# Two graph layers on one core: contraction rows in another order, one row per step, and the second half of the gather ahead of the sums

## The chip, the cores and the metric

The program runs on one core of a Trainium2 chip. The metric is device time in microseconds (us) of one execution; lower is better. All operands are fp32.

## What is computed

```python
# N = 3327 nodes, D = 512; adj is dense in memory, [N, N]
h = relu(layernorm(x))                              # layer 0
q, k, v = h @ Wq.T + bq, h @ Wk.T + bk, h @ Wv.T + bv
x = x + softmax(q @ k.T / sqrt(D) + 2 * adj) @ v
h = relu(layernorm(x))                              # layer 1
A2 = adj + I
s = diagonal(A2) ** -0.5
x = x + relu((s[:, None] * A2 * s[None, :]) @ (A2 @ h @ W.T))
```

## The kernel before, in words

**Tiles.** The 3327 rows are padded to 26 tiles of 128. Large products are done by a Strassen scheme of seven products ("p1" to "p7", in the order p5, p1, p6, p7, p2, p3, p4, line 30), so both the contraction rows and the output columns are cut into halves. Columns stand in two strips (line 38): strip 0 has tiles 0 to 13, strip 1 tiles 14 to 25, and each strip has an upper half y=0 (7 or 6 tiles, 896 or 768 columns) and a lower half y=1. Contraction rows are tiles 0 to 12 in the first half and 13 to 25 in the second.

**Start (lines 266 to 374).** Each tile of x is normalised and transposed in four packs, its rows are stored to `rowd[0]`, and queries are projected and stored to `qd`.

**Scores (lines 379 to 568).** Four groups of 13 steps make exp(scores). Each step loads a tile row of adj (`adjacency`), and `sum_of_adjacency` also stores two sums of adj's quarters, with ones added on the diagonal (line 439), for the second layer. The order on DVE, PE, POOL and SP is the program's own there (`in_order`); what is issued outside it, such as the first loads of the layers, is placed by a planner that goes by estimated times.

**The three passes (lines 923 to 1039).** Pass g=0 is exp(scores) @ h, pass 1 is A2 @ h1, pass 2 is A2 @ temp. A pass is 7 products x 2 strips x 7 steps. The text writes a step as (g, product, strip, t), t = 0 to 5 or None; a product's strip is 896 or 768 columns wide and each matmul takes half of that, 448 or 384. Steps t = 0 to 5 multiply two contraction tiles at once by seven matmuls of one more Strassen level (`Step.multiply`, line 772); the odd thirteenth tile is step None, with four plain matmuls (line 764). PSUM has 8 banks: seven accumulate p1 to p7 of the inner level. Bank 3 serves the rows described below. In step None the fourth matmul, "p8", goes into p1's bank.

What step k of `run` (line 1006) issues, in order: the loads of step k+3 (SP queue); the matmuls of step k; on DVE the sums for step k+2 (`four_sums`, lines 170 to 172, three instructions); after t=5 `Gather.first` (lines 800 to 804), which copies p1 on ACT and empties p6, p7, p5 on DVE; in step None `Gather.rest` (lines 817 to 820), which empties p2, p3, p4 and p8 on DVE, and `settle` (lines 822 to 833), two DVE instructions for products p6, p2, p3, p4 and six for p7; then what `between` holds for the step. All five engines run in the order in which this is written. Step (…, 0) of the next product and strip starts each bank anew and so waits until `first` and `rest` have read it; its order is p6, p7, p5, p2, p3, p4, p1, and in other steps p1 comes first. The second matmul of those steps reads the third of the sums, written at line 171.

`between` holds: loads of the right operands five steps ahead (SP) and their differences three steps ahead (DVE, lines 176 to 179 and 734 to 740), for the first product p5 of passes 1 and 2 three and two steps ahead; `Job`s, 52 sums for later S2 and S4 (line 855); and the **rows**. A row of pass 0 is one finished output tile: four matmuls with Wv into bank 3 (line 864), on DVE x + product / total (876), + bias (877), statistics (190 to 194); a store of the new x by POOL (878); one step later the relu on ACT into an `h1` tile (883) and its store by POOL to `rowd[1]` (884). Its x tile is loaded one step ahead on ACT's queue (871) into one of three places; `h1` has two. A row of pass 1 is four matmuls with W (864), a scaling on ACT (892) and a store. Rows of pass 2 (`finish`) are transposed, scaled, added to x and stored out (917 to 920).

**When rows come before.** Outputs of the upper half y=0 are final after product p3, those of y=1 after p4. Rows 0 to 3 stand in steps (g, p3, 1, 2 to 5), rows 4, 5, 6, 14, 15, 16 in (g, p4, 0, 0 to 5), rows 7; 8, 9; 10; 11, 12; 13 in (g, p4, 1, 1 to 5), two in one step twice, and rows 20 to 25 and 17 to 19 in every second step from (g+1, p5, 0, 0). Product p5 of the next pass needs contraction tiles 0 to 12 alone.

**Diagonal.** `left` (line 679) loads the left operand. For A11, A12 and A22 of passes 1 and 2 it comes from adj, and ones are added on its diagonal by DVE right behind the load's issue (line 696), three steps before use.

Of the kernel before, what the change touches and what calls it, by code (L numbers as in the profile page):

```python
# [15 lines left out]
P = 128  # L16
# [19 lines left out]
HALF = 13  # L36
PAIRS = 6
STRIPS = (0, 14)
HT = (7, 6)
H = tuple(n * P for n in HT)  # L40
Q = tuple(n * P // 2 for n in HT)


@with_exitstack
def graph_layers_kernel(
# [28 lines left out]
    nc = tc.nc  # L74
# [193 lines left out]

    def load_x(i, queue=nc.sync):
        xt = x_ring([P, D], "xt")  # L270
        queue.dma_start(xt, x[i * P : (i + 1) * P])
        return xt

    order = [(k, t + y * HALF) for k in TURN for t in range(PACKS[k][0], sum(PACKS[k])) for y in range(2)]
# [36 lines left out]
    def h_transposed(k):  # L311

        a, n = PACKS[k]
        for _, i in (o for o in order if o[0] == k):
            xt = first.pop(i) if i in first else load_x(i)
            rstd, bias = norm(xt)
            ht = n_ring([P, D], "ht")
            nc.scalar.activation(ht, xt, AF.Relu, bias=bias(), scale=rstd)
            nc.gpsimd.dma_start(rowd[0][i], ht)
            pt = tp_bank("tp").rearrange("p (c e) -> p c e", c=DC)  # L320
            for c in range(DC):
                nc.tensor.transpose(pt[:, c], ht[:, c * P : (c + 1) * P], ident)
            w = slice((i % HALF - a) * P, (i % HALF - a + 1) * P)
            if i < HALF:
                nc.scalar.copy(hp[k][:, 0:2, :, w], pt.rearrange("p (a c) e -> p a c e", a=2))
            else:
                nc.scalar.copy(hp[k][:, 2, :, w], pt[:, 2:4])
                nc.vector.tensor_add(hp[k][:, 3, :, w], hp[k][:, 2, :, w], pt[:, 0:2])
                nc.vector.tensor_add(hp[k][:, 5, :, w], hp[k][:, 0, :, w], pt[:, 0:2])
        nc.vector.tensor_add(hp[k][:, 4], hp[k][:, 3], hp[k][:, 0])  # L330
        nc.vector.tensor_add(hp[k][:, 6], hp[k][:, 1], hp[k][:, 4])

    def project_q(k):
        a, n = PACKS[k]
        w = n * P

        qs = [half(8 + j, [P, 2, BW], "qs") for j in range(4)]

        def chain(o):
            def product(ps, name, start):  # L340
                for c in range(2):
                    nc.tensor.matmul(ps[:, :w], M[B[name]][:, c, o * P : (o + 1) * P], hp[k][:, A[name], c],
                                     start=start and c == 0, stop=c == 1, skip_group_check=True)

            def first(j, ps, sign):
                d = 2 * (j % 2) + o
                nc.scalar.activation(qs[j][:, o, :w], ps[:, :w], AF.Identity, bias=u[:, d : d + 1], scale=float(sign))

            def more(j, ps):
                nc.vector.tensor_add(qs[j][:, o, :w], qs[j][:, o, :w], ps[:, :w])  # L350

            def last():
                if o == 1:
                    for j in range(4):
                        y, z = divmod(j, 2)
                        i = (y * HALF + a) * P
                        nc.gpsimd.dma_start(qd[:, 2 * z : 2 * z + 2, i : i + w], qs[j][:, :, :w])

            Chain(product, first, more, last)

        for o in range(2):
            chain(o)
# [43 lines left out]
    def adjacency(s, q, t):  # L406

        wd, c = Q[s], q * Q[s]
        g = [take([P, 2, Q[0]], f"g{k}")[:, :, :wd] for k, take in enumerate(g_rings)]
        for k in range(2):  # L410
            r0, c0 = (k * HALF + t) * P, STRIPS[s] * P
            src = adjT[r0 : r0 + P, c0 : c0 + 2 * H[s]].rearrange("p (y w) -> p y w", y=2)
            nc.sync.dma_start(g[k], src[:, :, c : c + wd])
        return g

    class Pair:
# [11 lines left out]
        def sum_of_adjacency(self, m):  # L428

            g, t, s = self.g, self.t, self.s  # L430
            if m == 0:
                self.o = o_ring([P, 2, Q[0]], "o")[:, :, : self.wd]
            o = self.o[:, m]
            parts = ((0, 0), (0, 1)) if m == 0 else ((1, 1), (0, 1))
            nc.vector.tensor_add(o, *(g[k][:, y] for k, y in parts))  # L435
            for k, y in parts:
                d = diagonal(o, (k * HALF + t) * P, STRIPS[s] * P + y * H[s] + self.c)
                if d:
                    nc.vector.tensor_add(o[:, d[0]], o[:, d[0]], d[1])
            if m == 1:  # L440
                nc.gpsimd.dma_start(self.to(sumd)[:, 0:2], self.o)  # L441
# [227 lines left out]

    spare = [(mid, k) for k in range(10, 15)]  # L670
    job_ring = ring(*spare[2:], (half, 14))
    h_ring = ring(*spare[:2])
    ts_ring = ring(*spare[:3])
    xr_ring = ring(*spare[:3], (half, 14))
    out_ring = ring((half, 12), (half, 13), *spare[3:])
# [3 lines left out]
    def left(g, s, what, t):  # L679


        js = [HALF - 1] if t is None else [t, t + PAIRS]
        a = a_ring().rearrange("p a w -> p (a w)")[:, : len(js) * H[s]].rearrange("p (k w) -> p k w", k=len(js))
        for k, j in enumerate(js):
            if g == 0:
                nc.sync.dma_start(a[:, k], pd[s][j][:, E_AT[what], :])
                continue
            if what in SUMS:
                nc.sync.dma_start(a[:, k], sumd[s][j][:, SUMS.index(what), :])
                continue  # L690
            y, z = int(what[1]) - 1, int(what[2]) - 1
            r0, c0 = (z * HALF + j) * P, STRIPS[s] * P + y * H[s]
            nc.sync.dma_start(a[:, k], adjT[r0 : r0 + P, c0 : c0 + H[s]])
            d = diagonal(a[:, k], r0, c0)
            if d:
                nc.vector.tensor_add(a[:, k, d[0]], a[:, k, d[0]], d[1])
        return a.rearrange("p k (y w) -> p k y w", y=2)

    class Right:

# [8 lines left out]
        def rows(self, dst, h, z):  # L709

            for k, i in enumerate(self.its):
                src = rowd[self.g][h * HALF + i]
                nc.sync.dma_start(dst[:, k], src if z is None else src[:, z * E : (z + 1) * E])

        def load(self):
# [29 lines left out]
    class Step:  # L745
# [3 lines left out]
            self.g, self.r, self.s, self.t, self.right = g, r, s, t, right  # L749

        def load(self):
            self.a = left(self.g, self.s, A_OF[self.r], self.t)

        def sums(self):
            if self.t is None:
                return
            self.o = o_ring3()[:, :, : Q[self.s]]
            four_sums(self.o, self.a.rearrange("p k y w -> p (k y) w"))
# [81 lines left out]
    class Job:  # L840
# [5 lines left out]
        def load(self):  # L846
            s, j, w = self.s, self.j, H[self.s]
            self.a, self.b = (job_ring([P, H[0]], "job")[:, :w] for _ in range(2))
            r0, c0 = (self.k * HALF + j) * P, STRIPS[s] * P
            nc.sync.dma_start(self.a, sumd[s][j][:, 1 + self.k])  # L850
            nc.sync.dma_start(self.b, adjT[r0 : r0 + P, c0 : c0 + w])
            self.d = diagonal(self.b, r0, c0)
# [14 lines left out]
    xts = {}  # L867

    def attend_load(i):
        xts[i] = view(2, 1).rearrange("p a w -> p (a w)")[:, len(xts) % 3 * D :][:, :D]  # L870
        nc.scalar.dma_start(xts[i], x[i * P : (i + 1) * P])

    def attend(i):
# [58 lines left out]
    def at(k, what, *args):  # L932
        between.setdefault(k, []).append((what, args))

    early = []
    for g in range(3):
        for n, r in enumerate(ORDER):
            for t, e in enumerate(every):
                k = number_of(g, n, 0, t)
                rh = rights[g, r, e]  # L940

                lead, make = (3, 2) if g and n == 0 else (5, 3)
                for what, when in ((rh.load, k - lead), (rh.make, k - make)):
                    if when < 0:
                        early.append(what)
                    else:
                        at(when, what)
# [8 lines left out]
    def rows(g, k, i, *z):  # L956

        if g == 0:
            at(k - 1, attend_load, i)
            at(k, attend, i)  # L960
            at(k + 1, attended, i)
        elif g == 1:
# [3 lines left out]
            at(k, finish, i, *z)  # L966


    for g in range(2):
        for t, i in {2: 0, 3: 1, 4: 2, 5: 3}.items():  # L970
            rows(g, number_of(g, 5, 1, t), i)
        for t, i in enumerate((4, 5, 6, 14, 15, 16)):
            rows(g, number_of(g, 6, 0, t), i)
        for t, its in {1: (7,), 2: (8, 9), 3: (10,), 4: (11, 12), 5: (13,)}.items():
            for i in its:
                rows(g, number_of(g, 6, 1, t), i)
        for k, i in enumerate((*range(20, 26), *range(17, 20))):
            rows(g, number_of(g + 1, 0, 0, 0) + 2 * k, i)
    within = {}
    for (n, s, t), its in {  # L980
# [25 lines left out]
    def run(k):  # L1006
# [13 lines left out]
        for j, _ in enumerate(step.multiply(banks_of)):  # L1020
            if j == 3 and t == PAIRS - 1 and gatherer.last:
                gatherer.first(banks_of)
            for what, args in within.get(k, ()) if j == 3 else ():
                what(*args)
        sums()
        if t == PAIRS - 1 and not gatherer.last:
            gatherer.first(banks_of)
        if t is None:
            gatherer.rest(banks_of)
            gatherer.settle()  # L1030
        for what, args in between.get(k, ()):
            what(*args)
# [382 lines left out]
```

## Time and profile before

| what | value |
|---|---|
| four runs | 2218.8, 2221.76, 2222.26, 2222.41 us; median 2222.01 |
| the profiled execution | 2222.17 us; span of its instructions 2220.3 us |
| granted TensorE clock, mean | 0.994 |
| DVE busy | 1618.5 us (73%) |
| ACT busy, POOL busy | 231.7 us (10%), 357.6 us (16%) |
| HBM traffic | 262 GB/s over the span |
| start and projections | 0 to about 120 us |
| scores | about 121 to 655 us |
| pass 0, 1, 2 | from about 642, 1158 and 1705 us |

In the profile, PE is the matmul engine and PEld its weight loads; an fp32 matmul leaves two records, so 14 records are one step of seven matmuls. A line of the timeline or of the groups gives start, duration, engine, source line, output<-inputs and count, and in brackets the idle time of that engine just before it and who ended it. DVE instructions overlap a little, so distances between starts are used below where a sum of work is meant.

### The profile page before, as it was taken

The page shows a single profiled execution, that of the slowest core. Times are in us where ns is not written, and L with a number is a line of the kernel's source. Part 1 is how long each engine was busy: PE and PEld are TensorE (multiplying, and loading weights), DVE is VectorE, ACT ScalarE, POOL GpSimd, SP SyncE. Part 2 cuts the span into 40 slices and gives each one's busy share as a digit, 9 for nine tenths or more (in the row PEclk, how much of TensorE's full clock was granted, in tenths as well). Part 3 has the DMA queues.
Part 4 walks back from the last instruction along what each step waited for, and adds up shares of the span by engine and source line. Part 5 has one row for each costly group of instructions (what it writes and reads, how often), then busy time and mean ns, then how long its engine had stood idle before and what let it go on. Part 6 is the DMA issues. An engine that isn't in the chain of part 4 may idle for free.

```text
span 2220.3 us, 20949 instructions
## 1 busy us (share of the span) xinstructions
PE 2179.7 (98%) x6268; PEld 1167.5 (53%) x6268; DVE 1618.5 (73%) x3092; ACT 231.7 (10%) x336; POOL 357.6 (16%) x551
## 2 busy tenths in 40 slices
PE   9999999999999999999999999999999999999997
PEld 5555555455555555555445555555554555555554
DVE  6369888788877789867767778986634457777675
ACT  5321111112110000000000000000000000000011
POOL 4223333333331000001222110000000000000011
PEclk9999999999999999999999999999999999999998
DMA  7568888888969898888787899886636458766684
GB/s 249 206 212 303 294 299 284 303 285 309 349 221 318 312 371 299 287 298 285 253 285 266 306 333 362 281 285 199 221 119 204 144 175 292 245 203 195 206 297 161
DMA packets 246682, 583.68 MB, mean 263 GB/s; under 512 B 34768, under 2 KB 106270, under 8 KB 246558
## 3 DMA queue, kind: packets, MB, share of 16 engines
q1 hardware_dynamic: 192270, 399.28, 54.2%
q0 software_dynamic: 44928, 167.49, 19.9%
q10 hardware_dynamic: 9360, 15.47, 2.1%
q8 instruction: 52, 0.85, 0.2%
q14 instruction: 72, 0.59, 0.1%
HBM read 414.28 MB, written 167.85 MB: 262 GB/s over the span
## 4 chain that ended last, share of the span: by engine, by line
PE 64%; DVE 3%; DMA 1%; issue 1%; ACT 0%; POOL 0%; ACTq 0%; SPq 0%; DVEq 0%; POOLq 0%
PE p L772 52%; PE p L864 8%; PE p L764 4%; DVE part L170 0%; PE pt L917 0%; DMA part<-in_x_dram 0%; DMA xr<-x1d 0%; DVE part L171 0%; DVE part L876 0%; DMA b<-row 0%; DVE part L172 0%; DMA rows<-row 0%; DMA part<-sum 0%; DVE st L190 0%; DVE part L877 0%
## 5 line engine op out<-in xcount | busy, mean ns | idle before, releaser
L772 PE MATMUL p<-part,b 128*128 128x448 f32 (+1 forms) x3528 | 1255.0, 514 | 7.9 <-DVE part L817 7.6
L772 PEld LDWEIGHTS p<-part,b 128*128 128x128 f32 x3528 | 668.8, 190 | 573.4 <-issue 307.1
L170 DVE TENSOR_TENSOR part<-part 128x896 f32<-128x896 f32 (+1 forms) x252 | 256.7, 1019 | 124.3 <-PE p L772 83.0
L449 PE MATMUL Y<-qt,hp 128*128 128x448 f32 (+1 forms) x832 | 309.0, 514 | 3.6 <-DVE g L453 2.6
L449 PEld LDWEIGHTS Y<-qt,hp 128*128 128x128 f32 x832 | 157.4, 190 | 139.1 <-issue 72.3
L449 PE MATMUL Z<-qt,hp 128*128 128x384 f32 (+1 forms) x416 | 162.6, 513 | 0.0
L172 DVE TENSOR_TENSOR part<-part,part 128x448 f32<-128x448 f32 (+1 forms) x219 | 129.5, 591 | 17.0 <-PE p L772 0.9
L171 DVE TENSOR_TENSOR part<-part,part 128x448 f32<-128x448 f32 (+1 forms) x219 | 129.4, 591 | 7.4
L864 PE MATMUL p<-w,ct 128*128 128x512 f32 x272 | 123.8, 594 | 3.9 <-DVE part L876 2.2
L764 PE MATMUL p<-part,b 128*128 128x448 f32 (+1 forms) x336 | 124.2, 513 | 0.0
L449 PEld LDWEIGHTS Z<-qt,hp 128*128 128x128 f32 x416 | 78.8, 190 | 67.4 <-issue 36.2
L453 DVE SCALAR_TENSOR_TENSOR g<-g,Y 128x384 f32<-128x384 f32 (+1 forms) x156 | 91.3, 585 | 27.3 <-PE Y L449 26.2
L858 POOL DMA_DIRECT2D sum<-job x52 | 28.4, 547 | 472.9 <-DVE job L855 260.7
L801 DVE TENSOR_TENSOR part<-p,part 128x384 f32<-128x384 f32 (+1 forms) x33 | 19.3, 586 | 103.9 <-PE p L772 103.3
L764 PEld LDWEIGHTS p<-part,b 128*128 128x128 f32 x336 | 63.6, 190 | 54.0 <-issue 33.0
L800 ACT COPY part<-p 128x384 f32<-128x384 f32 (+1 forms) x33 | 16.6, 503 | 682.3 <-PE p L772 681.5
L864 PEld LDWEIGHTS p<-w,ct 128*128 128x128 f32 x272 | 51.3, 190 | 64.7 <-issue 50.5
L449 PE MATMUL X<-qt,hp 128*128 128x384 f32 (+1 forms) x208 | 81.1, 512 | 0.0
L456 ACT ACTIVATE g<-g 128x768 f32<-128x768 f32 (+1 forms) x48 | 43.0, 896 | 352.0 <-DVE g L453 300.4
L441 POOL DMA_DIRECT2D sum<-o x52 | 36.9, 709 | 219.9 <-DVE o L435 153.9
L864 PE MATMUL p<-w,part 128*128 128x512 f32 x144 | 65.7, 592 | 0.0
L876 DVE SCALAR_TENSOR_TENSOR part<-p,rs,part 128x512 f32<-128x512 f32 x26 | 19.5, 750 | 62.9 <-PE p L864 47.3
(162 smaller groups left out, 1872.7 us busy)
## 6 DMA issues: line engine op xcount, KB each, us to landing
part<-sum SPq DMA_DIRECT2D x104, 448.0 KB, 4.9
part<-p SPq DMA_DIRECT2D x91, 448.0 KB, 6.2
part<-sum SPq DMA_DIRECT2D x104, 384.0 KB, 3.5
part<-p SPq DMA_DIRECT2D x91, 384.0 KB, 4.1
part<-in_adjT_dram SPq DMA_DIRECT2D x78, 448.0 KB, 4.7
b<-row SPq DMA_DIRECT2D x234, 128.0 KB, 4.8
part<-in_adjT_dram SPq DMA_DIRECT2D x78, 384.0 KB, 3.7
g<-in_adjT_dram SPq DMA_DIRECT2D x52, 448.0 KB, 4.6
```

What stands on the lines that cost most here:

```text
L170: nc.vector.tensor_add(o[:, 0:2], g[:, 0:4:3], g[:, 1:2].to_broadcast([P, 2, g.shape[-1]]))
L171: nc.vector.tensor_add(o[:, 2], o[:, 1], g[:, 0])
L172: nc.vector.tensor_add(o[:, 3], o[:, 2], g[:, 2])
L441: nc.gpsimd.dma_start(self.to(sumd)[:, 0:2], self.o)
L449: nc.tensor.matmul(ps[:, :wd], h_of(self.t, name, k), qt[B[name]][:, k], start=start and k == 0, stop=k == 1, skip_group_check=True)
L453: nc.vector.scalar_tensor_tensor(a[n], a[n], 2.0, ps[:, :wd], op0=ALU.mult, op1=ALU.add if sign > 0 else ALU.subtract)
L456: nc.scalar.activation(g[1], g[1], AF.Exp, **({"bias": pad} if self.t == HALF - 1 else {}))
L764: yield nc.tensor.matmul(ps[("p2", "p3", "p4", "p8")[k]][:, :w], b[:, z], a[:, 0, y], start=k == 3, stop=True)
L772: yield nc.tensor.matmul(ps[r][:, :w], b[:, i], m, start=self.t == 0, stop=self.t == PAIRS - 1 and r in ("p1", "p5", "p6", "p7"))
L858: nc.gpsimd.dma_start(sumd[self.s][self.j][:, 2 + self.k], self.a)
L864: nc.tensor.matmul(ps, cts[s][y][d][:, k * P : (k + 1) * P], w[d], start=d == 0, stop=d == DC - 1)
L876: nc.vector.scalar_tensor_tensor(xt, ps, rs[:, i : i + 1], xt, op0=ALU.mult, op1=ALU.add)
```

## The change

Five edits, all of them in the order of things; no matmul is added or removed.

```diff
+ROW = tuple(STRIPS[s] + y * HT[s] + k for y in range(2) for s in range(2) for k in range(HT[s]))
...
-        queue.dma_start(xt, x[i * P : (i + 1) * P])
+        queue.dma_start(xt, x[ROW[i] * P : (ROW[i] + 1) * P])
```

Contraction place i now stands for row tile `ROW[i]`: 0 to 6, 14 to 19 (all of y=0) in the first half, 7 to 13, 20 to 25 (all of y=1) in the second. Every address that names a contraction row (`rowd`, `qd`, adj's rows, the diagonal's place) goes through `ROW`.

```diff
-    h_ring = ring(*spare[:2])
+    x_slots = [lambda k=k: view(2, 1).rearrange("p a w -> p (a w)")[:, k * D : (k + 1) * D] for k in range(3)]
+    x_slots = itertools.cycle([*x_slots, lambda: mid(10, [P, D], "xt")])
+    h_ring = ring((mid, 11))
...
+        diagonals = []
...
             if d:
-                nc.vector.tensor_add(a[:, k, d[0]], a[:, k, d[0]], d[1])
-        return a.rearrange("p k (y w) -> p k y w", y=2)
+                diagonals.append((a[:, k, d[0]], d[1]))
+        return a.rearrange("p k (y w) -> p k y w", y=2), diagonals
...
         def sums(self):
+            for a, d in self.diagonals:
+                nc.vector.tensor_add(a, a, d)
             if self.t is None:
                 return
...
-        xts[i] = view(2, 1).rearrange("p a w -> p (a w)")[:, len(xts) % 3 * D :][:, :D]
+        xts[i] = next(x_slots)()
...
-                lead, make = (3, 2) if g and n == 0 else (5, 3)
-                for what, when in ((rh.load, k - lead), (rh.make, k - make)):
+                for what, when in ((rh.load, k - 5), (rh.make, k - 3)):
...
-            at(k - 1, attend_load, i)
+            at(k - 2, attend_load, i)
...
     for g in range(2):
-        for t, i in {2: 0, 3: 1, 4: 2, 5: 3}.items():
-            rows(g, number_of(g, 5, 1, t), i)
-        for t, i in enumerate((4, 5, 6, 14, 15, 16)):
-            rows(g, number_of(g, 6, 0, t), i)
-        for t, its in {1: (7,), 2: (8, 9), 3: (10,), 4: (11, 12), 5: (13,)}.items():
-            for i in its:
-                rows(g, number_of(g, 6, 1, t), i)
-        for k, i in enumerate((*range(20, 26), *range(17, 20))):
-            rows(g, number_of(g + 1, 0, 0, 0) + 2 * k, i)
+        k = number_of(g, 5, 1, 2)
+        for i in ROW:
+            if steps[k].t is None:
+                k += 1
+            rows(g, k, i)
+            k += 1
...
+        if t is None:
+            gatherer.rest(banks_of)
         sums()
         if t == PAIRS - 1 and not gatherer.last:
             gatherer.first(banks_of)
         if t is None:
-            gatherer.rest(banks_of)
             gatherer.settle()
```

So rows of passes 0 and 1 now stand one in each step t = 0 to 5 from (g, p3, 1, 2) to (g+1, p5, 1, 3); in step None DVE does rest, sums, settle instead of sums, rest, settle; the ones of the diagonal are added at the head of the sums, two steps before use; x is loaded two steps ahead into four places, one of them taken from `h1`, which keeps one; and p5's right operands of passes 1 and 2 are loaded and made as early as those of the other products.

More of the change, by code (lines that the diff above doesn't have):

```diff
@@ L318, in h_transposed @@
             nc.scalar.activation(ht, xt, AF.Relu, bias=bias(), scale=rstd)
-            nc.gpsimd.dma_start(rowd[0][i], ht)
+            nc.gpsimd.dma_start(rowd[0][ROW[i]], ht)
             pt = tp_bank("tp").rearrange("p (c e) -> p c e", c=DC)
@@ L355, in last @@
                         y, z = divmod(j, 2)
-                        i = (y * HALF + a) * P
+                        i = ROW[y * HALF + a] * P
                         nc.gpsimd.dma_start(qd[:, 2 * z : 2 * z + 2, i : i + w], qs[j][:, :, :w])
@@ L410, in adjacency @@
         for k in range(2):
-            r0, c0 = (k * HALF + t) * P, STRIPS[s] * P
+            r0, c0 = ROW[k * HALF + t] * P, STRIPS[s] * P
             src = adjT[r0 : r0 + P, c0 : c0 + 2 * H[s]].rearrange("p (y w) -> p y w", y=2)
@@ L436, in sum_of_adjacency @@
             for k, y in parts:
-                d = diagonal(o, (k * HALF + t) * P, STRIPS[s] * P + y * H[s] + self.c)
+                d = diagonal(o, ROW[k * HALF + t] * P, STRIPS[s] * P + y * H[s] + self.c)
                 if d:
@@ L691, in left @@
             y, z = int(what[1]) - 1, int(what[2]) - 1
-            r0, c0 = (z * HALF + j) * P, STRIPS[s] * P + y * H[s]
+            r0, c0 = ROW[z * HALF + j] * P, STRIPS[s] * P + y * H[s]
             nc.sync.dma_start(a[:, k], adjT[r0 : r0 + P, c0 : c0 + H[s]])
@@ L711, in rows @@
             for k, i in enumerate(self.its):
-                src = rowd[self.g][h * HALF + i]
+                src = rowd[self.g][ROW[h * HALF + i]]
                 nc.sync.dma_start(dst[:, k], src if z is None else src[:, z * E : (z + 1) * E])
@@ L751, in load @@
         def load(self):
-            self.a = left(self.g, self.s, A_OF[self.r], self.t)
+            self.a, self.diagonals = left(self.g, self.s, A_OF[self.r], self.t)
         def sums(self):
+            for a, d in self.diagonals:
+                nc.vector.tensor_add(a, a, d)
             if self.t is None:
@@ L848, in load @@
             self.a, self.b = (job_ring([P, H[0]], "job")[:, :w] for _ in range(2))
-            r0, c0 = (self.k * HALF + j) * P, STRIPS[s] * P
+            r0, c0 = ROW[self.k * HALF + j] * P, STRIPS[s] * P
             nc.sync.dma_start(self.a, sumd[s][j][:, 1 + self.k])
```

## The prediction

> **What bounds the kernel now.** I read the page's busy shares first, then who PE waited for, then PE's timeline at each wait, then DVE's timeline at the same places.
>
> ```profile
> PE 2179.7 (98%) x6268; PEld 1167.5 (53%) x6268; DVE 1618.5 (73%) x3092; ACT 231.7 (10%) x336; POOL 357.6 (16%) x551
> ```
>
> PE is the bound, and the change takes no matmul away. So only PE's waits can be won: 2220.3 - 2179.7 = 40.6 us, of which 14.2 are the tail after the last matmul. The list of PE's waits gives the rest:
>
> ```profile
> PE p L772 <- DVE part L817: 7.6, 5, 2.5
> PE p L864 <- DVE part L876: 2.2, 3, 0.8
> PE pt L917 <- DVE part L830: 2.2, 1, 2.2
> PE p L864 <- ACT ts L892: 1.7, 2, 0.8
> ```
>
> L817 is the first instruction of rest: a new product waits for the bank of p2. L876 and L892 read the rows' bank 3. In PE's timeline at the largest wait:
>
> ```profile
> 1158.72 2.42 PE L772 MATMUL p<-part,b 128*128 128x448 f32 x6
> 1163.67 4.97 PE L772 MATMUL p<-part,b 128*128 128x448 f32 x8 [2.54 <-DVE part L817]
> ```
>
> And in the table of windows, where the third column from the end is the granted clock:
>
> ```profile
> 1164.00:1167.00 3.00, 3.00 (x5) 1.35 (x5) 3.00 (x6) 0.00 (x0) 0.00 (x0) 0.50 0.99 384
> ```
>
> Three matmuls run, the fourth (p2) waits 2.54 us, and then eight records take 4.97 us. The window says why: the clock is 0.50. The same pair stands at 2132.49 (2.34 idle, then 4.97). After the 1.48 us wait at 1048.31 the eight records took 3.27, and unhindered ones 3.17. So a wait costs its printed time + 0.26 (0.10 of slower start, 0.16 by which ends overlap the next start), and the two longest cost 4.97 - 3.27 = 1.70 more for the clock.
>
> The Trainium skill, "TensorE: Matmul & The Clock Gate", Part 1, has the clock fall after an idle window of about 3.4 us. Here 2.34 us were enough, so the measurement decides; by the page alone the gain below would be 2 x 1.70 = 3.4 us smaller.
>
> **Rest ahead of the sums.** DVE at the same place:
>
> ```profile
> 1160.74 1.09 DVE L170 TENSOR_TENSOR part<-part 128x896 f32<-128x896 f32 x1
> 1161.86 0.63 DVE L171 TENSOR_TENSOR part<-part 128x448 f32<-128x448 f32 x1
> 1162.53 0.62 DVE L172 TENSOR_TENSOR part<-part 128x448 f32<-128x448 f32 x1
> 1163.07 0.55 DVE L817 TENSOR_TENSOR part<-part,p 128x384 f32<-128x384 f32 x1
> ```
>
> DVE reached step None late, and 2.33 us of sums (1163.07 - 1160.74; 2.06 when the sums are 384 wide) stand before the bank is read. Rest first frees p2 that much sooner. The waits on L817 are 1.48, 0.36, 2.54, 0.85 and 2.34, and one on its ct form is 0.21: 7.78 + 6 x 0.26 + 2 x 1.70 = 12.7 us. Two keep a remainder: at 1161, L817 would end at 1161.29 for a matmul due at 1161.13, and at 2130 at 2130.12 for 2130.16; with the restart, 0.45 and 0.3. Gain 12.0, and no clock fall.
>
> This edit has a price: until rest's products exist, DVE now stands still where it made sums. It shows where the sums of t=2, queued behind settle, were only just in time. The longest settle is p7's, six instructions. PE's timeline in pass 0, strip 0:
>
> ```profile
> 869.18 3.17 PE L764 MATMUL p<-part,b 128*128 128x448 f32 x8
> 872.19 14.18 PE L772 MATMUL p<-part,b 128*128 128x384 f32 x43
> ```
>
> and DVE's timeline beside it:
>
> ```profile
> 868.32 0.95 DVE L170 TENSOR_TENSOR part<-part 128x768 f32<-128x768 f32 x1
> ...
> 872.39 0.62 DVE L820 TENSOR_TENSOR part<-part,p 128x448 f32<-128x448 f32 x1
> ...
> 881.29 0.56 DVE L171 TENSOR_TENSOR part<-part,part 128x384 f32<-128x384 f32 x1
> ```
>
> Rest's last instruction (L820) starts when p8's product appears, 872.39, in either order. So the sums that began at 868.32 now begin behind it, and everything later on DVE shifts by 2.06. L171's sum ended at 881.85 and is due at 872.19 + 2 x 4.51 + 0.64 = 881.85 (two steps, one matmul). Loss 2.05. To cost nothing a sum must end 0.15 before its due start. The same sum for p7, strip 0 in passes 1 and 2: ready 1431.71, due 1432.59; ready 1972.90, due 1973.77; lead 0.88 and 0.87, so loss 2.05 - 0.73 = 1.3 each. For strip 1, where L817 did wait elsewhere, it began 0.84 after the step's first matmul (1593.08 after 1592.24), and the next three 0.645 apart. In pass 1 that puts rest's end at 1450.01 + 0.84 + 3 x 0.645 + 0.47 = 1453.25, the sums' at 1455.6 instead of 1454.45: shift 1.1, lead none (ready 1463.70, due 1463.86), loss 1.1. In pass 0 DVE is late there (sums at 900.75), shift 0.1, loss 0.1. In pass 2 the shift, 1.15, falls on the transposes that wait 2.16 us for settle's L830: loss 1.15, a wait of 3.3 us. Sum 2.05 + 1.3 + 1.3 + 1.1 + 0.1 + 1.15 = 7.0. Other steps None have two or no settle instructions and leads above 2 us. If one window holds enough of the 3.3 us wait the clock falls once more, 1.70; 2.16 there did not do it. I leave it out and keep it for the range.
>
> **Rows one per step.** Where two rows shared a step the second waited for bank 3: 0.84, 0.84 (DVE), 0.83, 0.83 (ACT). One per step leaves the reader a whole step: 3.34 + 4 x 0.26 = 4.4 gained. The new load fits: a 384-wide row step takes PE 4.51 + 3.43 = 7.94; DVE needs 2.06 sums, 2.53 row (0.78 + 0.72 + 0.73 + 0.30), 0.07, 1.66 differences and a 0.9 job in every third step: 7.2. Only t=5 with first (2.2) runs over; that is the 0.45 above. Rows now follow each other at (1, p5, 0, 0) and 1, where DVE comes from behind: 0.2 lost.
>
> **x two steps ahead.** The third L876 wait, 0.56, came after DVE had waited 2.08 for x, issued at 1053.28 and landed at 1059.93. A step more (8 us) covers the longest landing, 8.8. But DVE's own queue ends at 1058.73 and PE, no longer held 1.74 before, asks at 1058.54: 0.5 of 0.82 stays, gain 0.3. Other waits for x hid behind PE.
>
> **One h1 tile.** The relu of a row now waits for the store of the one before. The store's landing, from the view of line 884:
>
> ```profile
> DMA to landing us min/median/max: 2.8/6.6/8.2
> ```
>
> It is issued 1.04 after the relu starts: 3.8 / 7.6 / 9.2 us a turn against 7.94 (8.69 in wide steps). At the median nothing waits; nobody but ACT's queue stands behind it (the next x load with a step to spare, and the copy L800). Bounds: 0 at the median, +12 at the maximum (rival 2). I take 0, the median. The page "DMA: Bandwidth & Descriptors" of the Trainium skill, section on the anatomy of one DMA, puts a DMA's fixed part near 2 us; by that there would be no question at all, but the row is three times that.
>
> **Diagonal with the sums.** DVE waited 20.9 us in 7 places for the load under L696; no PE wait hangs on them, so nothing comes back. The new row order makes it 13 + 13 tiles a pass instead of 7 + 6 + 7: 12 more instructions at 0.2 apart, 2.4 us of DVE's slack. **p5's operands earlier**: two SP loads per step move up by two steps, as all other products have them, and the rows they need (tiles 0 to 12 of the new order) are stored by (g, p4, 1, 3). SP's waits in the passes are for PE to free a slot. 0.
>
> **Row order in scores.** 28 diagonal pieces instead of 29, but in group 4 the steps t=10 to 12 get two instead of one, on a DVE whose lateness shows as PE waits of 0.36 to 0.99 between 608 and 640: up to 3 x 0.2, I take 0.4. The planner may place the layers' first loads differently; the six waits from 581 to 653 sum to 4.24 + 6 x 0.26 = 5.8, so between -5.8 and +5.8, taken as 0, since their lengths and order do not change. Queries now need the second pack alone, but PE did not wait for them: 0.
>
> **Sum.** 12.0 + 4.4 + 0.3 - 0.2 - 7.0 - 0.4 = 9.1 us off the profiled execution's 2222.17 (span 2220.3 + 1.87 around it): 2213.1. That execution lies 0.16 above the median of 2222.01, within the runs' spread (2218.8 to 2222.41).
>
> **Rivals.** (1) *The price eats the gain.* The clock falls at the 3.3 us wait and at the 2.05 one (3.4 us), and scores lose 3 to the planner: 9.1 - 6.4 = 2.7 off, 2219.5. For it: DVE leads under 0.2 us at two of six places. Against: no wait of 2.16 or less has lowered the clock so far. (2) *Slower: the one h1 tile.* If stores land at 8.2 us throughout, ACT falls 9.24 - 7.94 = 1.3 us back per row; after the six rows of (0, p4, 1) it is 7.7 late. There first needs ACT's copy of p1; it stood ready 3.7 us before DVE came (1149.51, 1153.24), so 4 us reach PE, and by (1, p5, 1) some 8 more: +12, net 2225. It decides from landings of 7.3 us on average. For it: the 7 to 8.2 us landings around 1134 to 1160. Against: 2.8 to 5 in the wide steps. (3) *More gain*: DVE is early enough at all places, and half the scores' waits go: 9.1 + 2.9 + 1.1, 2208. (4) *The rows do not pull apart* because the next row's x or bank is late anyhow: the 4.7 of rows and x stay, 2217.8, a weaker form of (1).
>
> **Chances.** Forecast (2209.5 to 2216.5) 0.52; rivals 1 and 4 together 0.24; rival 2 0.10; rival 3 0.14. 0.2% (4.4 us) is about what measurement can tell. Faster: 0.52 + 0.14 + a third of 0.24 = 0.74; same 0.16; slower 0.10. The range leaves out rival 2 and the far end of rival 3: 2207 to 2221.
>
> **What the profile after should show.** No PE wait on L817 above 0.4; none on L892; no half clock near 1161 or 2130; new PE waits on L171 in the third step after p7's steps None, 1 to 2 us; the wait for L830 near 3.3; ACT's relu waiting for its store in under a third of the rows. Wrong would be: relu waits that grow from row to row, half-clock windows at the new waits, or longer waits before 655.

## The result, and the profile after

The changed kernel takes 2216.51 us (median of 36 runs, 2213.11 to 2223.88), the kernel before 2222.24 (57 runs, the first four among them). The ratio is 0.9978, with a 95% interval of 0.9973 to 0.9983. So by the ratio the change gains 4.9 us (3.8 to 6.0; the two medians stand 5.7 apart): faster by 0.2%, inside the range of 2207 to 2221, and little more than half of the 9.1 us that were forecast. The profiled execution took 2218.59 us (span 2216.8); it lies 2.1 above its median, so it shows only 3.5 of the gain.

Line numbers after are 8 higher in the passes and 3 higher in the scores: L780 is the L772 of before, L825 the L817, L838 the L830, L884 the L876, L452 the L449; the sums L170 to L172 are now L173 to L175, and L762 is the diagonal with the sums. The list of PE's waits, after:

```profile
PE p L780 <- DVE part L174: 4.9, 4, 1.9
PE Y L452 <- DVE g L456: 4.4, 5, 1.8
PE pt L925 <- DVE part L838: 3.1, 2, 2.5
...
PE p L780 <- DVE part L825: 1.6, 1, 1.6
...
PE p L598 <- DVE good L593: 0.6, 1, 0.6
PE p L872 <- DVE part L884: 0.4, 1, 0.4
```

Of the six waits on L817 (one in its ct form) one is left, and the four double-row waits (two on L876, two on L892) are gone. In their place stand four waits on the sums' second instruction (L174), a longer wait for settle (L838), one on L825, longer waits in the scores (L456), and 0.62 us for L593, an instruction of the check of the softmax totals. The first kind, in PE's timeline after p7's step None of pass 0, strip 0:

```profile
884.56 0.49 PE L780 MATMUL p<-part,b 128*128 128x384 f32 x1
886.97 3.49 PE L780 MATMUL p<-part,b 128*128 128x384 f32 x10 [1.93 <-DVE part L174]
```

and DVE beside it:

```profile
875.40 0.62 DVE L828 TENSOR_TENSOR part<-part,p 128x448 f32<-128x448 f32 x1
875.94 0.95 DVE L173 TENSOR_TENSOR part<-part 128x768 f32<-128x768 f32 x1
...
884.51 0.95 DVE L863 TENSOR_TENSOR job<-job 128x768 f32<-128x768 f32 x1
885.38 0.95 DVE L173 TENSOR_TENSOR part<-part 128x768 f32<-128x768 f32 x1
886.36 0.56 DVE L174 TENSOR_TENSOR part<-part,part 128x384 f32<-128x384 f32 x1
```

The reader is to see that DVE is never idle from 875.94 to 886.92: the sums of the step before wait behind rest (L828), then come six settle instructions and a job, and the sum that PE needs ends at 886.92. In strip 1 of pass 2 the transposes wait for the last of the six, with half the clock behind it; the timeline of PE:

```profile
1996.47 0.33 PE L925 MATMUL pt<-ident,part 128*128 128x128 f32 x1 [0.56 <-DVE part L838]
1999.32 0.47 PE L925 MATMUL pt<-ident,part 128*128 128x128 f32 x1 [2.52 <-DVE part L838]
1999.59 3.74 PE L780 MATMUL p<-part,b 128*128 128x448 f32 x6
```

and the table of windows there, the granted clock third from the end:

```profile
1996.00:1999.00 3.00, 0.33 (x1) 0.14 (x1) 2.93 (x4) 0.00 (x0) 0.00 (x0) 0.97 0.68 202
1999.00:2002.00 3.00, 2.68 (x5) 1.45 (x6) 2.90 (x8) 0.47 (x1) 0.00 (x0) 0.50 0.44 156
```

The steps None come in the same order in both kernels, so the starts of those steps can be compared one by one. Differences of these starts (after minus before), stage by stage:

| stretch | forecast | measured |
|---|---|---|
| start and scores, to the first step None (675.51, then 678.31) | +0.4 | +2.80 |
| turn at 680 | -0.5 | +0.2 |
| pass 0, p7, strips 0 and 1 | +2.05, +0.1 | +2.06, +0.06 |
| p4's and p5's turns, rows of pass 0, x | -9.8 | -9.63 |
| turn at 1390 (0.11 wait) | 0 | -0.37 |
| pass 1, p7, strips 0 and 1 | +1.3, +1.1 | +1.32, +1.13 |
| rows of pass 1 | -2.2 | -2.2 |
| pass 2, p7, strip 0 | +1.3 | +1.33 |
| pass 2, p7, strip 1 (transposes) | +1.15 | +2.54 |
| turn at 2130 | -4.0 | -2.40 |
| last step and tail | 0 | -0.4 |
| sum | -9.1 | -3.5 |

Three rows are off by more than 1 us: the start with the scores, the transposes, and the turn at 2130. The turn at 680 is off by 0.7: the wait on L817 there is gone, but PE waited 0.62 us for L593 at 691. Four of the nine profiles of the new order show that wait (0.36 to 1.35), none of the three of the old one; why is open.

### The profile page after: what moved, and what is told of

Same layout as the page of the kernel before. It is cut to its first block, busy times and chain, and to the rows that moved or that the text cites. A ratio compares the mean times of both kernels' runs of the same rounds, so it can differ in the third digit from the quotient of the medians.

```text
span 2216.8 us, 20976 instructions
## 1 busy us (share of the span) xinstructions
PE 2178.4 (98%) x6268; PEld 1167.7 (53%) x6268; DVE 1627.6 (73%) x3103; ACT 231.2 (10%) x336; POOL 356.4 (16%) x551
## 4 chain that ended last, share of the span: by engine, by line
PE 88%; DVE 4%; DMA 4%; issue 2%; POOL 0%; ACT 0%; SPq 0%; ACTq 0%; DVEq 0%; POOLq 0%
PE p L780 52%; PE Y L452 12%; PE p L872 7%; PE Z L452 6%; PE p L772 5%; PE X L452 3%; PE Y L345 2%; DMA g<-in_adjT_dram 1%; DMA xt<-in_x_dram 1%; DMA b<-row 1%; PE Z L345 1%; DVE part L173 1%; PE pt L925 0%; DVE part L174 0%; DMA xr<-x1d 0%
## 5 line engine op out<-in xcount | busy, mean ns | idle before, releaser
L780 PE MATMUL p<-part,b 128*128 128x448 f32 (+1 forms) x3528 | 1253.6, 513 | 6.7 <-DVE part L174 4.9
L780 PEld LDWEIGHTS p<-part,b 128*128 128x128 f32 x3528 | 668.4, 190 | 571.3 <-issue 307.4
L173 DVE TENSOR_TENSOR part<-part 128x896 f32<-128x896 f32 (+1 forms) x252 | 256.9, 1019 | 95.3 <-PE p L780 40.1
L452 PE MATMUL Y<-qt,hp 128*128 128x448 f32 (+1 forms) x832 | 309.5, 514 | 5.4 <-DVE g L456 4.4
L452 PEld LDWEIGHTS Y<-qt,hp 128*128 128x128 f32 x832 | 156.9, 190 | 141.8 <-issue 72.3
L452 PE MATMUL Z<-qt,hp 128*128 128x384 f32 (+1 forms) x416 | 162.5, 513 | 0.0
L175 DVE TENSOR_TENSOR part<-part,part 128x448 f32<-128x448 f32 (+1 forms) x219 | 129.5, 591 | 16.6 <-DVE part L174 0.5
L174 DVE TENSOR_TENSOR part<-part,part 128x448 f32<-128x448 f32 (+1 forms) x219 | 129.4, 591 | 7.4
L772 PE MATMUL p<-part,b 128*128 128x448 f32 (+1 forms) x336 | 124.2, 513 | 0.0
L452 PEld LDWEIGHTS Z<-qt,hp 128*128 128x128 f32 x416 | 78.8, 190 | 67.4 <-issue 37.2
L456 DVE SCALAR_TENSOR_TENSOR g<-g,Y 128x384 f32<-128x384 f32 (+1 forms) x156 | 91.3, 585 | 28.4 <-PE Y L452 27.7
L772 PEld LDWEIGHTS p<-part,b 128*128 128x128 f32 x336 | 63.6, 190 | 53.7 <-issue 32.6
L452 PE MATMUL X<-qt,hp 128*128 128x384 f32 (+1 forms) x208 | 81.1, 512 | 0.0
L92 POOL DMA_DIRECT2D out_dram<-r x30 | 16.3, 542 | 304.4 <-DVE r L928 269.2
```

The lines of the kernel that those rows point to most:

```text
L173: nc.vector.tensor_add(o[:, 0:2], g[:, 0:4:3], g[:, 1:2].to_broadcast([P, 2, g.shape[-1]]))
L174: nc.vector.tensor_add(o[:, 2], o[:, 1], g[:, 0])
L175: nc.vector.tensor_add(o[:, 3], o[:, 2], g[:, 2])
L452: nc.tensor.matmul(ps[:, :wd], h_of(self.t, name, k), qt[B[name]][:, k], start=start and k == 0, stop=k == 1, skip_group_check=True)
L456: nc.vector.scalar_tensor_tensor(a[n], a[n], 2.0, ps[:, :wd], op0=ALU.mult, op1=ALU.add if sign > 0 else ALU.subtract)
L772: yield nc.tensor.matmul(ps[("p2", "p3", "p4", "p8")[k]][:, :w], b[:, z], a[:, 0, y], start=k == 3, stop=True)
```

## The experiments

Nine further kernels ran, one of them (e8) twice. Ratios are to the kernel before, in runs on the same chip. "e3" and so on are the names of the kernels.

**e1: rest first alone, in the kernel before.**

```diff
+        if t is None:
+            gatherer.rest(banks_of)
         sums()
...
-            gatherer.rest(banks_of)
             gatherer.settle()
```

> The kernel before with one edit: rest ahead of the sums in every step None. My theory (by place): the L817 waits go (1.74 + 0.62 + 4.05 + 1.11 + 4.0 + 0.47 = 12.0), and p7's steps None lose what the changed kernel's profile shows there (2.05 at 885, 1.3 at 1428, 1.1 at 1460, 1.3 at 1969, 2.5 at 1996 with a fall of the clock = 8.3). Net 3.7 less than before, about 2218.5. The rows' waits of 0.84 and 0.83 stay, and at 2130, where the one added diagonal sum and the later xr of the changed kernel are absent, PE waits 0.3 or less. Rival A (the losses at p7 come from the new row order's loads and not from the sums' place): no L171 waits in the third steps after p7's steps None, 12 less than before, about 2210. Rival B (the lateness of the scores is due to chance): the scores, which are the same here as in the kernel before, may end up to 3 us later or earlier than at 641.99; by my theory they end within 0.7 of it.

Measured: 2222.64 us, ratio 1.0001 (0.9992 to 1.001). No gain can be told: the interval reaches from 1.8 us less to 2.2 more, so the 3.7 less that I expected is out. PE's waits:

```profile
PE p L772 <- DVE part L171: 4.9, 4, 1.9
PE p L864 <- DVE part L876: 3.9, 3, 2.2
...
PE pt L917 <- DVE part L830: 3.1, 2, 2.5
...
PE p L864 <- ACT ts L892: 1.7, 2, 0.8
PE p L864 <- DVE part L833: 1.3, 1, 1.3
```

The four waits on L171 and the 3.1 on L830 are those of the changed kernel to 0.01 us, without any of its other edits: rival A fell, the price at p7 belongs to the order of sums and rest. At 2130 PE does not wait (4.3 gained). But two waits that my theory lacked take the rest of the gain: 2.19 for the third row's x at 1062, with half the clock after it, and 1.31 at 1169 for settle (L833), whose result a row in p5's first step reads, and which PE now reaches without the wait at 1161 in front of it. The half-clock window at 884 (the changed kernel has none there) took 1.7 more. The scores ended at 641.99, as before.

**e2: the changed kernel with the sums first again.**

```diff
-        if t is None:
-            gatherer.rest(banks_of)
         sums()
...
+            gatherer.rest(banks_of)
             gatherer.settle()
```

> The changed kernel with rest put back behind the sums, so what is left is the row order with one row per step, x two steps ahead and the diagonal with the sums. My theory: rows and x gain 4.7, scores lose 2.5 to the new order, L817's waits stay (five of them, the two longest with half clock), no L174 waits after p7: 2 less than before, about 2220. Rival A: the L174 waits after p7 are still there, about 2228. Rival B: scores lose nothing on average, 4.7 less than before, 2217.5.

Measured: 2217.87 us, ratio 0.9981 (0.9972 to 0.999). That is nearer to rival B's 2217.5 than to my 2220, which lies at the interval's end: the scores ended 1.0 us later than before, not 2.5. No wait on L174: rival A fell again. And

```profile
PE p L780 <- DVE part L825: 8.4, 4, 4.0
```

with 2.0 more on the ct form (1.67, 0.37). So the rows, x and the diagonal alone give about 4.2 us, and rest first on top of them gives 0.7 (0.9981 to 0.9978), which the two intervals do not tell from nothing.

**e3: the changed kernel, but in p7's steps None the sums first.**

```diff
-        if t is None:
+        late = step.r == "p7"
+        if t is None and not late:
             gatherer.rest(banks_of)
         sums()
...
+        if t is None and late:
+            gatherer.rest(banks_of)
         if t is None:
             gatherer.settle()
```

> The changed kernel with the sums ahead of rest in p7's steps None alone, rest first in the other six products. My theory: the five losses at p7 (2.05 + 1.3 + 1.1 + 1.3 + 1.2 with its fall of the clock 1.4 more) come back and no L825 wait comes in their place, since the kernel before had none of its L817 waits there: 7 to 8.4 less than the changed kernel, about 2208.5, and the transposes at 1999 wait 2.2 again at full clock. Rival A (row order's loads): the same as the changed kernel, 2216.5. Rival C (a wait takes their place: p2's bank is now late for the p7 to p2 turn, because rows and the steps before have moved): L825 waits of up to 2 us at p7's steps None, 2212 or more.

Measured: 2206.89 us, ratio 0.9931 (0.9918 to 0.9945), 15.3 us less than before. No half-clock window is left in the passes before the tail, and PE's waits there are these:

```profile
PE pt L925 <- DVE part L838: 2.2, 1, 2.2
PE p L780 <- DVE part L825: 1.6, 2, 1.4
...
PE p L872 <- DVE part L884: 0.5, 1, 0.5
```

That is 9.6 us less than the changed kernel's median, a little more than the 7 to 8.4 expected; between the two profiles 8.6 of 9.0 us stand at p7. No L174 wait is left, and no L825 wait came at p7 (the two are 0.15 at 1155 and 1.43 at 2120): rival C fell. So about two thirds of what rest first wins (8.4 of 12) had been given back at one product of seven.

**e4: A2's diagonal added at its load again.**

```diff
-                diagonals.append((a[:, k, d[0]], d[1]))
+                nc.vector.tensor_add(a[:, k, d[0]], a[:, k, d[0]], d[1])
```

> The changed kernel with A2's diagonal piece added where its tile's load is issued, as before. My theory: of the 1.63 us that PE waits for L825 at 2130, 0.6 is the two diagonal pieces (0.49 + 0.1) that now stand ahead of the sums and the rest there, and 1.0 is DVE's late start on a row whose xr landed late; without the pieces the wait is about 1.0 and the time 0.6 less than the changed kernel's, which is near what these rounds can tell. DVE's waits for the adjacency load come back (20.9 us in the kernel before) with no wait of PE behind them. Rival: the diagonal with the sums is what buys the gain at the turns of pass 1, and PE waits of more than 0.5 come back between 1046 and 1260: 1 to 3 us more than the changed kernel.

Measured: 2217.83 us, ratio 0.9977 (0.9968 to 0.9986), the same as the changed kernel. No wait between 1046 and 1260 is above 0.5: the rival fell. The wait at 2130 is 0.85 instead of 1.63, near the 1.0 expected, but not for my reason. DVE's timeline there:

```profile
2123.20 0.69 DVE L928 TENSOR_TENSOR r<-r,xr 128x512 f32<-128x512 f32 x1 [2.53 <-DMA xr<-x1d]
```

Two pieces of later steps still stand between this and L825 (L702, at 2123.81 and 2131.10), and L825 starts at 2131.30: 8.10 us, as the changed kernel takes 8.03 (2122.42 to 2130.45). What differs is that the load of xr landed 6.68 us after its issue instead of 7.52. In e5 below, with the pieces at the sums, the load took 6.71 and the wait is 0.83. DVE's waits for the adjacency load came back and more (51.4 us in 13 places), with no wait of PE behind them. This edit of the change is worth nothing that can be measured.

**e5: e3 with x one step ahead.**

```diff
-            at(k - 2, attend_load, i)
+            at(k - 1, attend_load, i)
```

> The version with p7's sums first (e3), with x loaded one step ahead again and all else as there. With rest first alone (e1) the third row's first DVE operation came 2.19 us late on PE at 1062 and a half-clock window followed; in the changed kernel and in e3 the same wait is 0.45 to 0.47. Theory X (the earlier load is what lets rest first keep its gain there): a PE wait on L884 of 2.0 to 2.3 us near 1061, 1.7 us more than e3 without a fall of the clock and 3.4 with one: 2208.5 to 2210.5. Prediction's own size: 0.3 us, not to be told from e3's 2206.9.

Measured: 2216.13 us, ratio 0.9975 (0.9965 to 0.9986): 9 us more than e3, where theory X expected 1.7 to 3.4. There are two such waits, 1.65 at 1057 and 2.55 at 1165. At the second, ACT's timeline (ACTq is its queue, which issues the load):

```profile
1160.99 0.81 ACT L891 ACTIVATE h<-xt,nb,rstd 128x512 f32<-128x512 f32 x1 [9.35 <-DVE nb L203]
1161.07 0.85 ACTq L879 DMA_DIRECT2D part<-in_x_dram  x2
```

and DVE's:

```profile
1167.49 0.75 DVE L884 SCALAR_TENSOR_TENSOR part<-p,rs,part 128x512 f32<-128x512 f32 x1 [2.60 <-DMA part<-in_x_dram]
```

One step ahead, the load of a row's x stands on ACT's queue behind the relu of the row before, and that relu waits for DVE (nb, a statistic that stands behind settle and sums). The load is issued at 1161.07 and lands at 1167.38. The profiled execution was the fastest of eight (2211.71) and had no half clock at either place; the other runs, 2212.54 to 2218.77, are longer than its profile explains, so of the 9 us some 4 (the two waits) are shown, and where the rest went is open.

**e6 and e7: no diagonal in the scores' sums**, in e3 and in the kernel before.

```diff
-                d = diagonal(o, ROW[k * HALF + t] * P, STRIPS[s] * P + y * H[s] + self.c)
-                if d:
-                    nc.vector.tensor_add(o[:, d[0]], o[:, d[0]], d[1])
```

> The version with p7's sums first (e3), with the diagonal pieces of the scores' sums of adjacency left out (28 DVE instructions of 0.2 to 0.3 us; the output is then not the reference's). The scores ended at 643.0 to 645.6 in the four profiles with the new row order and at 641.99 in both with the old one. Theory D (two pieces in one step of the last group make DVE late): the scores end near 642 to 643, the waits on L456 at 582 to 613 shrink from 3 us to 1.5 or less, time 2204.5. Theory M (the adjacency rows in the new order land later, and DVE waits for them): the scores still end at 644 to 645.5, time as e3, 2206.9.

> The kernel before, with the 29 diagonal pieces of the scores' sums left out (the output is then not the reference's). It is the control for the run above. Theory D: the old order spreads its pieces one a step, they cost little, the scores end at 641 to 642, and the time is 0 to 1 less than before (2221.5 to 2222.4). Theory M: no change here either, 641.99. If the scores end as much earlier here as in the run above, the pieces cost the same in both orders, and the difference between the orders lies elsewhere.

Measured: e6 2211.03 us (ratio 0.9948, 0.9934 to 0.9961), scores ending at 645.17; e7 2223.07 (1.0, 0.9991 to 1.0009), at 641.46. Nothing speaks for theory D: without a single piece the scores still ended late in the new order. But it is one profile each, and e5's scores, with all pieces, ended at 641.64, so one profile decides little. (The old order is also no clean control: it has seven steps with two pieces, in groups 2 and 3.) That e6 is not faster than e3 (2206.89) fits. Why its median is 4 us higher is not settled: the intervals of the two ratios overlap, and e6's profile, 1.0 us longer than e3's, has two half-clock windows that e3's lacks (behind a 2.04 wait at 638 and the 2.17 one at 1989), 3.4 us.

**e8: e3 with two moves in the last pass.**

```diff
-                at(k - 1, finish_load, i)
+                at(k - (2 if n == 5 or (n, s) == (6, 0) and t < 2 else 1), finish_load, i)
...
-        rows(2, number_of(2, 4, 0, t), i, (1,))
+        rows(2, number_of(2, 4, 0, t) + 1, i, (1,))
```

> The version with p7's sums first (e3), with two further moves in the last pass: xr of the rows in p3's second strip and of p4's first two steps is loaded two steps ahead instead of one, and the half rows 20 to 25 are finished one step later, in steps 1 to 6 of p2 and not 0 to 5. My theory: DVE stands 3.8 us for xr before the turn at 2120, which is why PE waits 1.43 us for L825 there; with xr there early that wait is 0.3 or less. The transposes at 1989 no longer meet p7's settle: their 2.17 us go. Together 1.2 + 0.26 + 2.17 + 0.26 = 3.9 less than e3: 2203. Rival: the earlier loads hold up ACT's queue or the store's slots, and the wait moves to another turn of the last pass: 2206 or more.

Measured: 2205.23 us, ratio 0.992 (0.9907 to 0.9934); its repeat below 2205.62. Both waits are gone from the list. Between 700 us and the last transposes PE waits 0.46 (L884) and 0.15 (L825) in both profiles, and nowhere else above 0.13. The profiled span fell by 3.3 against e3's (2207.8 to 2204.5), the median by 1.7, where 3.9 was expected; the rival's 2206 was not reached. The two intervals overlap, so the times alone do not tell e8 from e3; the profiles do.

**e9: the scores' first queries held back, and e8 again beside it.**

```diff
+                if n == 0:
+                    nc.sync.dma_start(qt[2 * k + y][:, :, 0:1], qd[:, 2 * k : 2 * k + 2, y * H[0] : y * H[0] + 1])
                 nc.sync.dma_start(qt[2 * k + y], qd[:, 2 * k : 2 * k + 2, c : c + wd])
```

> The version with the earlier xr loads and the later finish (e8), with the loads of the scores' first queries held behind the store of the third pack by four small loads (one column each), so that the sign change of the first query tile stands behind the last packs' copies in ScalarE's order again, as in the kernel before. Theory Q (with the new row order the first queries need one pack alone, so their sign change is put ahead of the third pack's first copies on ScalarE, waits there for the store and the load of that pack, and PE behind it): the wait on L350 near 100 (0 to 1.4 us in the seven profiles of the new order, none in the three of the old one) is gone, the scores start 38.8 us after the last transpose, as in the three profiles of the old order, instead of 39.1 to 40.5; 1 to 1.7 less than e8, 2203.9. Rival: the later queries are late for the scores' first matmuls, which wait as much or more: 2205.2 or more, scores starting 40 us or more after the last transpose.

> The same as e8, beside e9 on the same chip, so that a difference of 1 to 2 us can be told. Theory Q: 1 to 1.7 more than e9, with a wait of 0.5 to 1.5 us on L350 near 100. Rival: equal to e9 or less. In both: no wait on L825 above 0.3 near 2117 and none on L838 near 1987.

Measured: 2205.04 us (0.9922, 0.9908 to 0.9936) and 2205.62 (0.9921, 0.9906 to 0.9935): equal, the rival's case. The wait on L350 is gone, as theory Q has it, but the scores' first matmuls now wait for the sign change itself, and start 40.8 us after the last transpose:

```profile
PE Y L454 <- ACT qt L408: 1.8, 1, 1.8
```

In e8's second profile the wait on L350 was 0.17, not the 0.5 to 1.5 expected. So the mechanism is there, its size changes from run to run, and the mend only moved it.

## Why the prediction was right in sign and too large in size

**The whole.** The sum had rest first at 12.0 - 7.0 = 5.0 net and the rows with x at 4.5. Measured, the rows, x and the diagonal alone give about 4.2 (e2), and rest first gives 0.7 on top of them and nothing alone (e1). So nearly all of the gain is the rows', and the edit that leads the prediction earned nothing that can be told: what it won at six products went at the seventh, at 2130 and to the clock. That the total still lies in the range is owed to the width of the range, 14 us, as much as to the working.

**Rest first: 12.0 for it, confirmed at every place but two.** At 1048, 1104, 1161 and 1254 the waits went as worked out (-9.63 against -9.8 with rows and x). At 680 the wait went, but the one on L593 came. At 2130 the step that failed was the remainder, "L817 would end ... at 2130.12 for 2130.16", with 0.3 left. L825 ended at 2130.99 for a matmul due 0.74 earlier than before. The load of xr and the instruction that waits for it, before:

```profile
2115.51 0.33 ACTq L900 DMA_DIRECT2D xr<-x1d  x1
2122.14 0.69 DVE L920 TENSOR_TENSOR r<-r,xr 128x512 f32<-128x512 f32 x1 [2.68 <-DMA xr<-x1d]
```

and after:

```profile
2114.77 0.33 ACTq L908 DMA_DIRECT2D xr<-x1d  x1
2122.42 0.69 DVE L928 TENSOR_TENSOR r<-r,xr 128x512 f32<-128x512 f32 x1 [3.82 <-DMA xr<-x1d]
2123.03 0.49 DVE L762 TENSOR_TENSOR part<-part,ident 128x128 f32<-128x128 f32 x2
...
2130.45 0.54 DVE L825 TENSOR_TENSOR part<-part,p 128x384 f32<-128x384 f32 x1
```

DVE left its wait for xr 1.0 later against PE (2122.42 instead of 2122.14, while PE came 0.74 earlier), and two diagonal pieces (0.6) stand behind it: from there to L825 DVE takes 8.03 us, and 7.44 from L920 to L817 in e1, which has no piece there. The working took DVE's chain to move with PE. The load's issue did, by 0.74; its landing did not, since the load took 7.52 us instead of 6.50. In all nine profiles with this load one step ahead it is issued 9.65 us before the step None, and in the new order with rest first there PE's wait follows its landing: 7.52 us and 1.63 of wait in the changed kernel, 7.31 and 1.43 in e3, 6.71 and 0.83 in e5, 6.68 and 0.85 in e4, 5.86 and none in e6. The passes of e3 and e6 are the same code, so one execution can differ from another by more than the 1.0 of this miss. Whether the new order also makes the load land later (5.86 to 7.52 us in six profiles, 6.22 to 6.50 in three of the old one) is open. The 0.6 of the pieces is the change's own. e8, with the load a step earlier, has no wait there.

**The price at p7: 7.0, measured 8.4**, and five of its six terms hit within 0.05 us. e1 shows that it belongs to this edit alone, e3 that it comes back whole. The one term too small is the transposes', 2.54 for 1.15: the waits grew by 0.9 (0.56 + 2.52 for 2.16), and the half clock took the rest. The step that failed is the half clock put at nothing: I had written "I leave it out and keep it for the range", because the 2.16 us wait before had not lowered the clock. It fell there in all three profiles with rest first at p7. Why 2.16 was no bound is told below.

**Rows one per step: 4.4, right.** No double-row wait is left.

**x two steps ahead: 0.3, mis-sized by its neighbour.** At 1062 the wait is 0.45, which with the restart of 0.26 is 0.71 where 0.5 was forecast. But 0.3 counts the edit beside the kernel before, and its worth depends on rest first: once PE is not held 1.74 us at the turn, an x loaded one step ahead is 2.19 late (e1), and e5 is 9 us slower than e3, of which the profile shows some 4.

**One h1 tile: 0, right.** The list of ACT's waits:

```profile
ACT h L891 <- DMA row<-h: 32.1, 5, 8.4
```

Five relus of 26 waited for the store, and no PE wait hangs on them; the slower rival did not come.

**Diagonal with the sums: 0**, right for the whole (e4). The pieces that the new row order adds were put at DVE's slack; at 2130 DVE had none, and they cost 0.6, at the load (e4) hardly less.

**Start and scores: +0.4, measured +2.8.** One part is named: "Queries now need the second pack alone, but PE did not wait for them: 0". PE did not, but ACT does. The planner, seeing the queries ready early, puts their sign change (L406) ahead of the copies that empty PE's banks. ACT's timeline after:

```profile
99.57 0.84 ACT L406 ACTIVATE qt<-qt 128x768 f32<-128x768 f32 x1 [4.70 <-DVE qt L179]
100.32 1.25 ACT L350 ACTIVATE qs<-Y,u 128x512 f32<-128x512 f32 x2
```

In the changed kernel's profile this costs PE only 0.03, but 1.25 in e3's, and up to 1.42 in the others. From the last transpose to the first score it took 38.8 us in all three profiles of the old order, and 39.1 to 40.5 in seven of the eight of the new one without e9's edit (38.8 in the eighth): 1.0 us more on average. Of the 2.8, though, 0.5 stood at the first score and 2.3 arose in the scores themselves. These took 520.4 to 522.4 us in the old order (three profiles) and 520.0 to 523.4 in the new (nine), so a difference of the orders can't be told from chance there. My 0.4 for two pieces a step is not shown (e6); how much later the scores end on average stays open.

**Rivals and signs.** Rival 1 came true in the profiled execution in two of its parts: the clock fell at the transposes, and start and scores lost 2.8; at the wait of 2.05 (measured 1.93) the clock did not fall, by luck of its place, as told below. Of the signs named, the waits on L171, the one for L830 (3.08 in two), L892 and the relus came as written; the 1.63 on L825 did not fit "above 0.4". Two signs of being wrong came: a half-clock window at a new wait, and longer waits before 655. Rival 3's sum is off: 9.1 + 2.9 + 1.1 less is 2209.1, not 2208.

## What to carry to other kernels

When an in-order queue is turned round, price each place where the queue runs for its slack: here one order was right at six products and wrong at the seventh, whose settle is three times as long, and a condition on that product was worth 10 us where the edit everywhere was worth 0.7, which the noise does not tell from nothing. A wait that goes uncovers the next one on the same path (a load that had been late all along), so two edits must be priced together, not each beside the kernel before. Where an engine's chain hangs on a load, the issue moves with the bound but the landing need not: here the same load took 5.9 to 7.5 us.

## What the runs showed of the hardware

The clock is judged in windows. In each of the twelve profiles all half-clock stretches begin on one grid of 3.413 us that runs through the execution (1998.82 in the changed kernel is 576 steps after 32.74, where the first one ends). Laid over PE's gaps, from the scores on: every window with 1.93 us or more of idle PE (13 of them) was followed by a window of half clock; of the 27 windows with 1.2 to 1.84 us only two were, both at the transposes of e4 (1.80, and 1.29 in a window itself at half clock). So what counts is whether about half of one window is idle, and where the wait falls on the grid: 1.93 us at 885 in the changed kernel was cut into 1.04 and 0.90 and cost nothing more, the same 1.93 in e1 lay in one window and cost 1.7; 2.55 in e5 was cut into 1.23 and 1.32 and cost nothing more; the 2.16 of before had been cut into 0.72 and 1.44. That wait, 2.16 or 2.17 at the transposes in six profiles, was followed by half clock in e5, e6 and e7 and not in the kernel before, e2 and e3. "TensorE: Matmul & The Clock Gate" of the Trainium skill, Part 1, has a window of this length that runs freely, which these traces agree with, and asks for an idle window before the clock falls; here half of one was enough. So by an estimate from these figures a wait of 1.9 to some 3.7 us (twice the 1.84 that one window bore) has a second price of 1.7 us that depends on its place on the grid. This may be part of why single executions of one kernel differ by some us; no two profiles of one kernel here show it.
